# An opening rearranged: the first batch found by its least key, one-hot tables in pieces, later gathers, and scores tied to their own banks

## The chip, the cores and the metric

The kernel runs on one core of a Trainium2 chip. The metric is the device time of one execution in microseconds (us), the median of several runs. TensorE is called PE (PEld for its weight loads), VectorE DVE, ScalarE ACT, GpSimd POOL and SyncE SP.

## What is computed

Sixteen batches of 1024 tokens with 512 channels go through an attention with 8 heads of 64, in which query, key and value are the same projection, and a 0/1 mask per token decides which tokens take part. The result passes through a second projection and is added to the input.

```python
def _L0_cond_ref(x, mask, Wq, Wo):            # x: (16, 512, 1024), mask: (16, 1024)
    xt = jnp.transpose(x, (0, 2, 1))
    q = xt @ Wq.T
    qh = q.reshape(B, T, NH, dk).transpose(0, 2, 1, 3)
    scores = scale * jnp.einsum('bhqd,bhkd->bhqk', qh, qh)
    logits = (scores * cmask + (1.0 - cmask) * NEG) * rmask
    attn = jax.nn.softmax(logits, axis=-1)
    ctx = jnp.einsum('bhqk,bhkd->bhqd', attn, qh)
    out = ctx @ Wo.T
return x + jnp.transpose(out, (0, 2, 1))
```

About half of the tokens of a batch are masked in. A row whose token is masked out has equal logits, so its context is the mean over all tokens.

## The kernel before

**Only masked-in tokens are worked on.** For each batch the kernel computes a slot for every token, turns the slots into a list of row numbers, and gathers the masked-in rows by an indirect DMA. Some 512 tokens per batch (512 for the first and the last two batches, 544 or 528 between, with the rest as padding) then go through the projection, the scores, the exponentials and the value product. The mean row for the masked-out tokens comes from sums over the batch's natural layout.

**Batches are taken in another order than they come.** `order` (L202 to L210) counts each batch's tokens on PE, makes a key of the count times 32 plus the batch's number, and ranks the keys by comparing all 16 with all 16. The batch of rank 15 (the comparison counts larger keys, so the least key) is taken first. `permute` (L224, L227) picks a batch's mask out of all by comparing ranks with the place (`placed`, L215). `sources` (L234 to L237) does the same for the batch's number, from which come the row numbers' base and the address of the natural layout.

**From a mask to gathered rows.** `slots_of` (L295 to L316) forms prefix sums of the mask on PE (L300, L304) and turns them into slots on DVE, and the token table `oht`. `hot` (L360) makes the one-hot table `tmp` of 8 blocks of 128 in one DVE instruction. `index` multiplies the two on PE (L369), and DVE writes the row numbers `idx` (L372) and two padding masks (L384, L386). `gather` issues an indirect DMA of 128 rows on POOL (L458), 256 KB each. `xt` transposes the gathered rows on PE (L562), ACT and DVE split them into a high and a low half-precision part (L520, L521).

**From rows to scores.** `query` runs 12 products of 128 by 256 (L591) into one PSUM buffer of `pm`, of which there are two, and ACT copies the result (L595). `qsplit` splits it on DVE (L614 to L616) and SP spreads it over the partitions with four DMAs (`xx`, L625 to L628). `value` transposes it (L651). `scores(b, p, u)` works on batch b, head pair p and half u of the rows: 8 products (L823) fill four PSUM banks, then four exponentials on ACT read one bank each (L838). The first product of the next scores waits for all four of them (`self.left`):

```python
            if n == 0 and self.left:
                self.needs(m.ins, *self.left)
```

`attend` multiplies the probabilities with the values (L858, 32 products per head pair) into banks 4 and 5.

**The order.** In the opening (up to `self.begun.close()`) the calls stand in a list `first`, written by hand, and the tile framework places instructions by priority; `behind` and `needs` add dependences. PE is fed with idle products (`warm`, L408) while it waits for rows. From then on, PE's order is the one in which the calls stand in `plan`, by step of the batch. Where `self.paced` is set, gathers and scatters go into a queue, and each step issues one to two of them, held back to the last PE instruction so far (`self.beat`). Loads of weights and of the natural layout are issued by SP, whose instructions run in order, as do those of each engine.

In the opening before, batch 0 and batch 1 are both prepared first (`order`, `permute`, `sources(0, 2)`, `slots_of(0)`, `hot(0)`, `index(0)`, four gathers, then `permute(1, 2)`, `slots_of(1)`). Batch 1's index and its first four gathers stand in `first` between the first queries of batch 0.

Of the kernel before, what the change touches and what calls it, by code (L numbers as in the profile page):

```python
# [15 lines left out]
ALU = mybir.AluOpType  # L16
# [31 lines left out]
class Fast:  # L48
# [47 lines left out]
    def setup(self, mask_t):  # L96
# [44 lines left out]
        self.act16 = fixed("act16", [P, B, TB], F16)  # L141
        self.rank = fixed("rank", [P, B])
        self.base = fixed("base", [P, B])
        self.first_row = fixed("first_row", [1, B], I32)
# [53 lines left out]
    def order(self):  # L198

        nc, B = self.nc, self.B  # L200
        mh = self.given16
        nc.vector.tensor_scalar(mh, self.mt, 0.5, None, ALU.is_gt)  # L202
        pn = self.pm([P, B])
        for j in range(TB):
            nc.tensor.matmul(pn, lhsT=self.on16, rhs=mh[:, :, j], start=(j == 0), stop=(j == TB - 1))
        key = self.sb([P, B], F32, "sc", 3)
        nc.vector.scalar_tensor_tensor(key, pn, 32.0, self.number, ALU.mult, ALU.add)
        more = self.sb([P, B, B], F16, "c", 4)
        nc.vector.tensor_tensor(more, key.unsqueeze(1).broadcast_to([P, B, B]), key.unsqueeze(2).broadcast_to([P, B, B]), ALU.is_gt)
        nc.vector.tensor_reduce(self.rank, more, AX.X, ALU.add)  # L210
# [75 lines left out]
    def slots_of(self, b):  # L286


        nc = self.nc
        n = self.n[:, b:b + 1]  # L290
        mb = self.act16[:, b]
        whole, half = self.sb([P, 7, TB], F32, "c", 4), self.sb([P, TB, 2 * NB], F16, "c", 4)
        free, sign, put, base, slot, hi, far = (whole[:, k] for k in range(7))
# [12 lines left out]
        nc.vector.scalar_tensor_tensor(base, free, n, put, ALU.mult, ALU.add)  # L306
        nc.vector.tensor_tensor(slot, sign, pr, ALU.mult)
        nc.vector.tensor_tensor(slot, slot, base, ALU.add)
        nc.vector.tensor_tensor(ge, slot.unsqueeze(2).broadcast_to([P, TB, NB - 1]),
                                self.kk_kept.unsqueeze(1).broadcast_to([P, TB, NB - 1]), ALU.is_ge)  # L310
        nc.vector.scalar_tensor_tensor(far, ge[:, :, 4], float(5 * P - C), slot, ALU.mult, ALU.add)
        nc.vector.tensor_reduce(hi, ge, AX.X, ALU.add)
        nc.vector.scalar_tensor_tensor(self.lo[:, b], hi, -float(P), far, ALU.mult, ALU.add)
        nc.vector.tensor_tensor(oh, hi.unsqueeze(2).broadcast_to([P, TB, NB]),
                                self.ionb.unsqueeze(1).broadcast_to([P, TB, NB]), ALU.is_equal)
        nc.vector.tensor_tensor(self.oht[:, b], oh, self.tok.unsqueeze(2).broadcast_to([P, TB, NB]), ALU.mult)  # L316

# [470 lines left out]
    def scores(self, b, p, u):  # L788
# [26 lines left out]
        for j in range(max(map(len, lanes))):  # L815
            calls += [l[j] for l in lanes if j < len(l)]
        opening = b == 0 and p == 0 and u == 0
        if opening:
            calls.sort(key=lambda c: c[0] // (2 * A))
        banks = [c[0] // 512 for c in calls]  # L820
        for n, (c0, c1, w, x) in enumerate(calls):
            with self.behind(*last), self.tc.high_priority(offset=HPO if n else 0):
                m = nc.tensor.matmul(flat[:, c0:c1], lhsT=w, rhs=x, start=banks[n] not in banks[:n], stop=banks[n] not in banks[n + 1:])  # L823
            if out and banks[n] < 4:
                self.other_banks(m.ins, out)
            elif out and banks[n] not in banks[:n]:
                self.needs(m.ins, out)
            self.other_banks(m.ins, *self.spot_reads)
            if n == 0 and self.left:
                self.needs(m.ins, *self.left)  # L830
            last = [m.ins]
        self.beat = last[0]
        self.left, self.context_out = [], None
        ps = {}
        for j in (0, 1, 2, 3) if opening else (3, 0, 1, 2):
            k, i, at = places[j]
            t = self.sb([P, C], F32, "p", 12)[:, :A]
            e = nc.scalar.activation(t, flat[:, at:at + A], AF.Exp, bias=s["nm"][p // 2][:, p % 2 * 2 + k:p % 2 * 2 + k + 1],  # L838
                                     scale=SCALE, accum_out=s["z"][:, 2 * p + k, i:i + 1]).ins
            self.exp = [e]  # L840
            self.left.append(e)
            ps[k, i] = t
        s.setdefault("p", {}).setdefault(p, {}).update(ps)

    def attend(self, b, p, after=None):
# [7 lines left out]
        for g in (1, 0):  # L853
            cols = slice(g * CH, (g + 1) * CH)
            for i in range(3, -1, -1):
                for k in (1, 0):
                    with self.behind(*(first or ([after] if after else []))), self.tc.high_priority(offset=HPO):
                        mm = nc.tensor.matmul(pav[k * DK:(k + 1) * DK, g], lhsT=s["v"][p][:, i, k * DK:(k + 1) * DK],  # L858
                                              rhs=ps[k, i][:, cols], start=(i == 3), stop=(i == 0 and A == 512))
                    self.other_banks(mm.ins, *exps[1 - g:])  # L860
                    if g == 0 and i == 3:
                        self.needs(mm.ins, *exps[:1])
# [231 lines left out]
    def run(self, flag):  # L1094
# [128 lines left out]
        if True:  # L1223
            stack = ExitStack()
            for b in range(B + 1):
# [23 lines left out]
                if n < B:  # L1249
# [57 lines left out]
                for k, x in enumerate([x for x in (b + 2, self.extra.get(b + 2)) if x is not None and x < B]):  # L1307
# [186 lines left out]
```

## Time and profile before

| | us |
|---|---|
| three runs | 964.02, 964.62, 966.39 |
| median | 964.62 |
| the profiled execution | 965.21 |
| its span, first to last instruction | 963.5 |
| busy in the span: PE, DVE, ACT, POOL | 931.5, 721.1, 644.7, 305.1 |

A row of the timeline reads: start, duration, engine, line and operation, output and inputs with their shapes, count, and in brackets how long the engine was idle before it and what ended that. The waits list who waited for whom, with the total, the number of times and the longest. A row by stage gives the stage, its length, the busy time of each engine with the number of instructions, the clock granted to PE as a share, the DMA engines' share and the GB/s that they moved. An instruction's duration includes its latency: on DVE the next independent one starts some 0.1 us before the end that is shown.

### The profile page before, as it was taken

Reading aid. Unit: us, or ns where it says so; the run is one execution under the profiler, and the core shown is the slowest. Engines: PE = TensorE matmul, PEld = TensorE weight load, DVE = VectorE, ACT = ScalarE, POOL = GpSimd, SP = SyncE. Lnnn points to the kernel's source line nnn. Section 1 sums busy time; section 2 is a strip of 40 time slices with the busy share of each in tenths; the row PEclk is TensorE's granted clock in tenths of the full one; section 3 lists DMA queues with packets and bytes.
Section 4 is the critical chain, followed back from the end, with each engine's and each line's share of the span. In section 5 each row is a group of like instructions: output and inputs, shape, how many; then the busy total and the mean of one; then the engine's idle time right before and its main releaser. Section 6 shows DMA issues by size and latency. Waiting matters only on the chain.

```text
span 963.5 us, 22790 instructions
## 1 busy us (share of the span) xinstructions
PE 931.5 (97%) x8121; PEld 581.3 (60%) x8121; DVE 721.1 (75%) x2443; ACT 644.7 (67%) x1669; POOL 305.1 (32%) x311
## 2 busy tenths in 40 slices
PE   6799999999999999999999999999999999999997
PEld 4556656566666666666666566666666666565543
DVE  7779677776777767887678687877877788685563
ACT  4778766667677666776767678665767866665651
POOL 2102022142241513415144250522515135252452
PEclk9999999999999999999999999999999999999999
DMA  5756556556675666756656787654767757555552
GB/s 172 222 175 203 155 154 183 163 180 190 180 209 148 194 197 193 220 157 199 177 181 204 198 239 223 177 158 136 214 168 233 243 144 207 151 161 161 171 175 102
DMA packets 78568, 176.30 MB, mean 183 GB/s; under 512 B 14480, under 2 KB 22416, under 8 KB 78448
## 3 DMA queue, kind: packets, MB, share of 16 engines
q1 hardware_dynamic: 57392, 107.09, 39.8%
q0 software_dynamic: 21056, 67.68, 22.4%
q8 instruction: 66, 1.08, 0.5%
q14 instruction: 54, 0.44, 0.2%
HBM read 91.36 MB, written 33.91 MB: 130 GB/s over the span
## 4 chain that ended last, share of the span: by engine, by line
PE 81%; DVE 10%; ACT 4%; DMA 2%; issue 2%; SPq 1%; POOL 0%; POOLq 0%; DVEq 0%; ACTq 0%
PE pss L858 22%; PE pss L823 17%; PE pm L982 17%; PE pm L591 16%; ACT p L838 2%; PE pss L876 2%; PE pm L562 2%; DMA xx<-hl 1%; PE pss L766 1%; PE pm L654 1%; DVE xl L521 1%; PE pss L982 1%; DVE xa L988 1%; PE pm L912 1%; DVE p L777 1%
## 5 line engine op out<-in xcount | busy, mean ns | idle before, releaser
L838 ACT ACTIVATE p<-pss,nm 128x528 f32<-128x528 f32 (+2 forms) x512 | 353.9, 702 | 104.7 <-PE pss L823 101.5
L858 PE MATMUL pss<-p,v 128*64 128x264 f32 (+2 forms) x2048 | 242.4, 389 | 0.0
L823 PE MATMUL pss<-xx 128*128 128x118 f16 (+17 forms) x1856 | 213.6, 287 | 3.9 <-ACT p L838 2.8
L1051 POOL DMA_INDIRECT y_out<-xa,idx x68 | 82.0, 1206 | 405.2 <-DVE nq L732 85.1
L858 PEld LDWEIGHTS pss<-p,v 128*64 128x64 f32 x2048 | 141.4, 137 | 85.8 <-issue 4.9
L823 PEld LDWEIGHTS <-xx 128*128 128x128 f16 (+1 forms) x1856 | 103.2, 96 | 85.1 <-issue 34.3
L591 PE MATMUL pm<-xh,wqh 128*128 128x264 f16 (+5 forms) x512 | 141.8, 277 | 3.3 <-DVE xl L521 1.3
L591 PE MATMUL pm<-xh,wql 128*128 128x264 f16 (+5 forms) x512 | 141.1, 275 | 0.0
L591 PE MATMUL pm<-xl,wqh 128*128 128x264 f16 (+5 forms) x512 | 140.9, 275 | 0.0
L591 PEld LDWEIGHTS <-wqh 128*128 128x128 f16 x1024 | 96.4, 97 | 31.6 <-issue 12.6
L458 POOL DMA_INDIRECT xa<-x_in,idx x68 | 72.5, 1066 | 123.4 <-DMA y_out<-xa,idx 49.1
L838 ACT ACTIVATION_READ_ACCUMULATOR p<-pss,nm 128x1 f32 x512 | 105.2, 205 | 0.0
L982 PE MATMUL pm<-woh,ch 128*128 128x512 f16 x240 | 91.1, 380 | 0.0
L982 PE MATMUL pm<-woh,cl 128*128 128x512 f16 x240 | 90.9, 379 | 0.0
L982 PE MATMUL pm<-wol,ch 128*128 128x512 f16 x240 | 90.9, 379 | 0.0
L595 ACT ACTIVATE q<-pm 128x264 f32<-128x264 f32 (+5 forms) x128 | 50.8, 397 | 43.1 <-PE pm L591 42.7
L988 DVE SCALAR_TENSOR_TENSOR xa<-pm,xa 128x512 f32<-128x512 f32 x61 | 41.6, 681 | 46.0 <-PE pm L982 45.7
L1051 POOL DMA_INDIRECT y_out<-xi,idx x60 | 64.9, 1081 | 33.9 <-PE pss L766 13.4
L658 ACT COPY v<-pm 128x512 f32<-128x512 f32 x64 | 37.5, 586 | 56.0 <-PE pm L654 54.3
L982 PEld LDWEIGHTS <-ch 128*128 128x128 f16 x480 | 44.9, 98 | 47.5 <-issue 4.1
L458 POOL DMA_INDIRECT xi<-x_in,idx x60 | 59.4, 990 | 21.6 <-issue 15.8
L881 ACT COPY c<-pss 128x528 f32<-128x528 f32 (+2 forms) x64 | 38.3, 598 | 37.9 <-PE pss L876 26.8
(249 smaller groups left out, 1485.0 us busy)
## 6 DMA issues: line engine op xcount, KB each, us to landing
xm<-x_nat_in SPq DMA_DIRECT2D x60, 512.0 KB
xx<-hl SPq DMA_DIRECT2D x208, 136.0 KB
rb<-rd SPq DMA_DIRECT2D x72, 132.0 KB
xx<-hl SPq DMA_DIRECT2D x48, 128.0 KB
pt<-c SPq DMA_DIRECT2D x36, 132.0 KB
pt<-p SPq DMA_DIRECT2D x36, 132.0 KB
rb<-rd SPq DMA_DIRECT2D x32, 136.0 KB
ub<-ud SPq DMA_DIRECT2D x16, 256.0 KB
```

Source lines behind the costliest of these rows:

```text
L458: dma = self.nc.gpsimd.indirect_dma_start(out=tile[:n], out_offset=None, in_=self.x, in_offset=bass.IndirectOffsetOnAxis(ap=idx, axis=0))
L562: self.pe = nc.tensor.transpose(pt[:, c, :], x[:n, c * P:(c + 1) * P], self.ident[:n, :n]).ins
L591: self.beat = nc.tensor.matmul(pq, lhsT=w[:, c, e * P:(e + 1) * P], rhs=xx[:, c, cols], start=(k == 0), stop=(k == 3 * DC - 1)).ins
L595: nc.scalar.activation(s["q"][:, e, cols], pq, AF.Copy, scale=1.0 / (SX * SW))
L658: nc.scalar.copy(v, pv)
L823: m = nc.tensor.matmul(flat[:, c0:c1], lhsT=w, rhs=x, start=banks[n] not in banks[:n], stop=banks[n] not in banks[n + 1:])
L838: e = nc.scalar.activation(t, flat[:, at:at + A], AF.Exp, bias=s["nm"][p // 2][:, p % 2 * 2 + k:p % 2 * 2 + k + 1], scale=SCALE, accum_out ...
L858: mm = nc.tensor.matmul(pav[k * DK:(k + 1) * DK, g], lhsT=s["v"][p][:, i, k * DK:(k + 1) * DK], rhs=ps[k, i][:, cols], start=(i == 3), sto ...
L881: self.context_out = nc.scalar.copy(c[:, :A].rearrange("p (g c) -> p g c", g=2), pav).ins
L982: mm = nc.tensor.matmul(po[:cols.stop - cols.start], lhsT=a[:, e, cols], rhs=w[:, e, :], start=(e == 0 and k == 0), stop=(e == DC - 1 and ...
L988: return self.nc.vector.scalar_tensor_tensor(x, po, 1.0 / (SX * SW), x, ALU.mult, ALU.add).ins
L1051: dma = self.nc.gpsimd.indirect_dma_start(out=self.out, out_offset=bass.IndirectOffsetOnAxis(ap=idx, axis=0), in_=x, in_offset=None)
```

## The change

Four things are changed, all in the preparation and the work of batch 0 and in the preparation of batch 1.

1. `order` ends with the least of the 16 keys per partition; comparing the keys with it picks the first batch's mask directly. The comparison of all keys and the ranks (`ranks`) come later, and `sources` runs for batches 1 to 15 alone. The first batch's number is the least key minus 32 times its count, in `slots_of`.
2. `slots_of` now makes the one-hot table itself, with a DVE instruction for each block of 128, and forms the token table after the third. `hot` is no longer called for batches 0 and 1.
3. Batch 1's slots stand behind the second block of transposes, its index behind the first value block and the split of the first query, and all five of its gathers in the queue of the first step, behind the first scores. The weights of the second projection and the natural layout of later batches are held back to `self.beat` in place of the instruction `top` of batch 0's first shift. Four of batch 1's five blocks of transposes, in place of three, stand ahead of the first `attend`.
4. In batch 0, a score product waits for the exponential that reads its own bank, and an exponential for the products of its own bank; the exponentials are taken in the order in which the banks are complete. `attend` no longer waits for the bank-3 exponential where a row of scores has 512 columns.

The number of idle products on PE goes from 30 to 24.

```diff
     def order(self):
...
-        key = self.sb([P, B], F32, "sc", 3)
+        key = self.fixed("key", [P, B])
         nc.vector.scalar_tensor_tensor(key, pn, 32.0, self.number, ALU.mult, ALU.add)
+        self.key = key
+        nc.vector.tensor_reduce(self.least, key, AX.X, ALU.min)
+        each = self.sb([P, TB, B], F16, "hl", 2)
+        nc.vector.scalar_tensor_tensor(each, key.unsqueeze(1).broadcast_to([P, TB, B]), self.least,
+                                       mh.rearrange("p b j -> p j b"), ALU.is_equal, ALU.mult)
...
+            nc.vector.tensor_reduce(self.act16[:, 0], each, AX.X, ALU.add)
+
+    def ranks(self):
+        nc, B, key = self.nc, self.B, self.key
         more = self.sb([P, B, B], F16, "c", 4)
...
     def slots_of(self, b):
...
+        if b == 0:
+            who = self.base[:, 0:1]
+            nc.vector.scalar_tensor_tensor(who, n, -32.0, self.least, ALU.mult, ALU.add)
+            nc.vector.tensor_copy(self.first_row[:, 0:1], who[0:1, :])
+            nc.vector.tensor_scalar(who, who, float(T), None, ALU.mult)
...
-        nc.vector.tensor_tensor(self.oht[:, b], oh, self.tok.unsqueeze(2).broadcast_to([P, TB, NB]), ALU.mult)
+        for j in range(TB):
+            nc.vector.tensor_scalar(ol[:, j], self.io128, lo[:, j:j + 1], None, ALU.is_equal)
+            if j == 2:
+                nc.vector.tensor_tensor(self.oht[:, b], oh, self.tok.unsqueeze(2).broadcast_to([P, TB, NB]), ALU.mult)
...
     def scores(self, b, p, u):
...
-            if n == 0 and self.left:
+            if alone and self.left:
+                own = (1, 2, 3, 0)[banks[n]]
+                if banks[n] not in banks[:n]:
+                    self.needs(m.ins, self.left[own])
+                self.other_banks(m.ins, *(e for k, e in enumerate(self.left) if k != own))
+            elif n == 0 and self.left:
                 self.needs(m.ins, *self.left)
...
-        for j in (0, 1, 2, 3) if opening else (3, 0, 1, 2):
+        for j in done:
...
+            if alone:
+                self.other_banks(e, *(m for m, bank in zip(mms, banks) if bank != j))
...
     def attend(self, b, p, after=None):
...
-                    self.other_banks(mm.ins, *exps[1 - g:])
-                    if g == 0 and i == 3:
+                    self.other_banks(mm.ins, *exps[(1 - g) * (self.reach > 512):])
+                    if g == 0 and i == 3 and self.reach > 512:
                         self.needs(mm.ins, *exps[:1])
...
     def run(self, flag):
...
             self.order()
-            self.permute(0, 1)
-            self.active(0, 1)
-            self.sources(0, 2)
             self.slots_of(0)
-            self.hot(0)
-        self.warm(6)
+        self.warm(5)
         self.index(0)
         for j in range(4):
             self.gather(0, j)
-        self.warm(5)
+        self.warm(13)
         with self.behind(self.st[0]["at"], self.pe):
-            with self.tc.high_priority(offset=HPO):
-                self.permute(1, 2)
-                self.active(1, 2)
-                self.slots_of(1)
             for f in halves:
                 f()
-            with self.tc.high_priority(offset=HPO):
-                self.sources(2, B)
+            self.ranks()
+            self.permute(1, 2)
             self.setup2()
-        self.warm(13)
...
             self.warm(2)
+            if k == 1:
+                self.slots_of(1)
...
         def index1():
             with self.behind(self.last_xs):
-                self.hot(1)
+                self.sources(1, B)
                 self.index(1)
...
-        first = query(0, 0, 0) + xt(0)[3:] + [(0, L(self.facts, 0, 2))] + query(0, 1, 0) + query(0, 0, 1)
+        first = query(0, 0, 0) + xt(0)[3:] + query(0, 1, 0) + query(0, 0, 1)
...
-        first += [(0, index1)] + sums0[:4] + value(0, 0) + g1[:1] + query(0, 1, 1)[:1] + g1[1:2]
-        first += value(0, 1) + split1 + sums0[4:] + query(0, 2, 0) + g1[2:3] + query(0, 2, 1)[:1] + g1[3:4]
+        first += sums0[:4] + value(0, 0) + query(0, 1, 1)[:1] + [(0, index1), (0, L(self.facts, 0, 2))]
+        first += value(0, 1) + split1 + sums0[4:] + query(0, 2, 0) + query(0, 2, 1)[:1]
...
-                        plan = {(0, 0): g1[4:] + query(0, 3, 0) + value(0, 2) + rng0,
+                        plan = {(0, 0): g1 + query(0, 3, 0) + value(0, 2) + rng0,
                                 (3, 0): query(0, 3, 1) + x[:1] + value(0, 3) + pk(b, 1),
-                                (5, 0): x[1:3], (5, 1): x[3:],
+                                (5, 0): x[1:4], (5, 1): x[4:],
...
-                        free.setdefault(2, []).append(L(self.load, "o", c, None, first_top))
+                        free.setdefault(4, []).append(lambda c=c: self.load("o", c, None, self.beat))
...
-                        free.setdefault(at, []).append(L(self.load_all, x, c, None if b else first_top))
+                        free.setdefault(at, []).append(L(self.load_all, x, c) if b else lambda x=x, c=c: self.load_all(x, c, self.beat))
```

More of the change, by code (lines that the diff above doesn't have):

```diff
@@ L142, in setup @@
         self.rank = fixed("rank", [P, B])
+        self.least = fixed("least", [P, 1])
         self.base = fixed("base", [P, B])
@@ L205, in order @@
             nc.tensor.matmul(pn, lhsT=self.on16, rhs=mh[:, :, j], start=(j == 0), stop=(j == TB - 1))
-        key = self.sb([P, B], F32, "sc", 3)
+        key = self.fixed("key", [P, B])
         nc.vector.scalar_tensor_tensor(key, pn, 32.0, self.number, ALU.mult, ALU.add)
+        self.key = key
[3 more added lines that the diff above has]
+                                       mh.rearrange("p b j -> p j b"), ALU.is_equal, ALU.mult)
+        with nc.allow_low_precision(reason="one of the terms is 0 or 1, the others are 0"):
+            nc.vector.tensor_reduce(self.act16[:, 0], each, AX.X, ALU.add)
+    def ranks(self):
+        nc, B, key = self.nc, self.B, self.key
         more = self.sb([P, B, B], F16, "c", 4)
@@ L291, in slots_of @@
         mb = self.act16[:, b]
-        whole, half = self.sb([P, 7, TB], F32, "c", 4), self.sb([P, TB, 2 * NB], F16, "c", 4)
-        free, sign, put, base, slot, hi, far = (whole[:, k] for k in range(7))
+        whole, half = self.sb([P, 8, TB], F32, "c", 4), self.sb([P, TB, 2 * NB], F16, "c", 4)
+        free, sign, put, base, slot, hi, far, lo = (whole[:, k] for k in range(8))
         ge, oh = half[:, :, :NB - 1], half[:, :, NB:]
@@ L312, in slots_of @@
         nc.vector.tensor_reduce(hi, ge, AX.X, ALU.add)
-        nc.vector.scalar_tensor_tensor(self.lo[:, b], hi, -float(P), far, ALU.mult, ALU.add)
+        nc.vector.scalar_tensor_tensor(lo, hi, -float(P), far, ALU.mult, ALU.add)
+        ol = self.st[b]["ol"] = self.sb([P, TB, P], F16, "tmp", 2)
         nc.vector.tensor_tensor(oh, hi.unsqueeze(2).broadcast_to([P, TB, NB]),
                                 self.ionb.unsqueeze(1).broadcast_to([P, TB, NB]), ALU.is_equal)
-        nc.vector.tensor_tensor(self.oht[:, b], oh, self.tok.unsqueeze(2).broadcast_to([P, TB, NB]), ALU.mult)
+        for j in range(TB):
+            nc.vector.tensor_scalar(ol[:, j], self.io128, lo[:, j:j + 1], None, ALU.is_equal)
+            if j == 2:
+                nc.vector.tensor_tensor(self.oht[:, b], oh, self.tok.unsqueeze(2).broadcast_to([P, TB, NB]), ALU.mult)
     def facts(self, b0, b1):
@@ L816, in scores @@
             calls += [l[j] for l in lanes if j < len(l)]
-        opening = b == 0 and p == 0 and u == 0
-        if opening:
+        alone = b == 0
+        if alone and p == 0 and u == 0:
             calls.sort(key=lambda c: c[0] // (2 * A))
-        banks = [c[0] // 512 for c in calls]
+        banks, mms = [c[0] // 512 for c in calls], []
         for n, (c0, c1, w, x) in enumerate(calls):
@@ L828, in scores @@
             self.other_banks(m.ins, *self.spot_reads)
-            if n == 0 and self.left:
+            if alone and self.left:
[4 more added lines that the diff above has]
+            elif n == 0 and self.left:
                 self.needs(m.ins, *self.left)
             last = [m.ins]
+            mms.append(m.ins)
         self.beat = last[0]
-        self.left, self.context_out = [], None
+        self.left, self.context_out, self.reach = [], None, A
+        done = sorted(range(4), key=lambda j: len(banks) - banks[::-1].index(j)) if alone else (3, 0, 1, 2)
         ps = {}
-        for j in (0, 1, 2, 3) if opening else (3, 0, 1, 2):
+        for j in done:
             k, i, at = places[j]
@@ L841, in scores @@
             self.left.append(e)
+            if alone:
+                self.other_banks(e, *(m for m, bank in zip(mms, banks) if bank != j))
             ps[k, i] = t
+        if alone:
+            self.left = [self.left[done.index(j)] for j in (3, 0, 1, 2)]
         s.setdefault("p", {}).setdefault(p, {}).update(ps)
```

## The prediction

> **What bounds the kernel now.** I read the page's totals first, then busy time by stage, then who waits for whom, and last the timelines of the first 52 us, queue by queue. All times are us from the start of the span; a batch's score step is written (batch, head pair, half).
>
> ```profile
> span 963.5 us, 22790 instructions
> PE 931.5 (97%) x8121; PEld 581.3 (60%) x8121; DVE 721.1 (75%) x2443; ACT 644.7 (67%) x1669; POOL 305.1 (32%) x311
> 30.00:40.00 10.00, 6.84 (x44) 3.52 (x44) 6.94 (x25) 6.23 (x20) 2.59 (x3) 1.00 1.03 277
> 40.00:52.00 12.00, 9.81 (x77) 6.17 (x75) 7.78 (x19) 9.59 (x26) 0.00 (x0) 1.00 0.61 183
> 52.00:63.00 11.00, 11.00 (x98) 6.94 (x96) 7.83 (x30) 8.60 (x24) 0.00 (x0) 1.00 0.59 183
> 63.00:100.00 37.00, 35.09 (x335) 22.37 (x333) 35.96 (x129) 30.70 (x80) 5.01 (x5) 1.00 0.67 193
> 140.00:963.50 823.50, 808.09 (x7072) 503.64 (x7070) 611.34 (x2054) 549.19 (x1423) 282.06 (x261) 1.00 0.63 183
> ```
>
> A stage row gives its length, then busy time of PE, weight loads, DVE, ACT, POOL, then clock, DMA share and GB/s. After 140, PE is busy 98% of the time, so the change cannot speed anything there; it can only bring the start of that stretch forward. Between 30 and 52 PE is busy 16.65 of 22: 5.35 us of idle PE lie in the stage that the change edits. From 52 to 63 PE has no gap at all, and from 63 to 100 DVE is full. So the question is when PE reaches the point 51.63 (step (0,1,1)), and whether DVE lets that shift pass.
>
> ```profile
> PE pss L823 <- ACT p L838: 2.3, 2, 1.8
> PE pm L651 <- ACT q L595: 1.2, 3, 0.6
> PE pm L912 <- DVE xl L521: 1.1, 1, 1.1
> PE pss L823 <- DMA xx<-hl: 1.0, 1, 1.0
> DVE sc L262 <- PE pm L256: 1.5, 1, 1.5
> ```
>
> These are PE's largest waits from 14 to 52, and DVE's wait for the slot products of batches 2 and 3, at the edge of its full stretch. Scores wait for exponentials (2.3), for the spread of the query (1.0), for buffers. DVE itself waited 1.5 us for PE just before its full stretch, so that stretch starts when PE lets it: a shift of PE passes on whole.
>
> **The change, step by step: up to the first index.**
>
> ```profile
> 4.67 0.42 DVE L209 TENSOR_TENSOR c<-sc 128x256 f16<-128x256 f32 x1
> 6.29 0.29 DVE L227 TENSOR_REDUCE act<-hl 128x8 f16<-128x128 f16 x1
> 8.58 1.22 DVE L360 TENSOR_TENSOR tmp<-io,lo 128x1024 f16<-128x1024 f16 x1
> 10.39 0.23 DVE L372 TENSOR_SCALAR idx<-pm,base 128x9 int32<-128x9 f32 x1 [0.45 <-PE pm L369]
> 10.62 0.28 DVE L384 TENSOR_SCALAR hr<-row,n 128x128 f32<-128x128 f32 x1
> 10.81 0.38 DVE L224 TENSOR_TENSOR hl<-c,given 128x128 f16<-128x128 f16 x1
> 16.38 1.09 DVE L194 SCALAR_TENSOR_TENSOR wql<-xa,wqh 128x256 f16<-128x256 f32 x3
> 7.05 2.72 PE L408 MATMUL warm<-on 128*128 128x512 f16 x6
> 12.75 2.97 PE L408 MATMUL warm<-on 128*128 128x512 f16 x13
> 16.42 0.60 PE L562 MATMUL pss<-ident,xa 128*128 128x128 f32 x4
> 19.06 0.27 PE L591 MATMUL pm<-xl,wqh 128*128 128x256 f16 x1
> 17.06 0.60 ACT L520 ACTIVATE xh<-pss 128x512 f16<-128x512 f32 x1 [0.27 <-PE pss L562]
> L458 POOL DMA_INDIRECT xa<-x_in,idx x4: 942/988/1299, 10.9 to 15.1; - x4
> DMA to landing us min/median/max: 3.5/3.5/3.5
> L458 POOL DMA_INDIRECT xa<-x_in,idx x4: 942/957/979, 24.9 to 31.8; - x4
> DMA to landing us min/median/max: 5.1/5.1/5.1
> ```
>
> *Least key for the ranking.* From L209 to the last reduction L227 pass 6.29-4.67 = 1.62 us. In their place stand a reduction of 16 elements and a compare-and-multiply of 128. The second is like L384 or L224 (0.28 to 0.38), the first no longer than L227; together about 0.6. Gain 1.0. The three small instructions for the batch number fall into gaps between dependent instructions: 0 to 0.2 lost; I take 0.
>
> *One-hot in pieces.* L360 writes 1024 elements in 1.22. Eight pieces of 128 follow each other at 0.19 if each goes like L384 (10.62 to 10.81), 1.5 in all, so 0.3 is lost; if a piece costs half of that, 0.4 is won. PE may multiply while the later pieces come, which saves most of the 0.45 that DVE waited before L372. Between -0.6 and +0.3; I take -0.1, because L384 is the nearest row. The index is then ready at 9.3 instead of 10.39. [...]
>
> *Gathers and the transposes.* POOL starts four gathers 1.4 apart (10.9 to 15.1) and each lands 3.5 later. Moved by 1.1, the first lands at 13.3. It now overlaps the natural-layout loads: 0 to 0.5 lost. PE's 13 warm products start at 9.35; six of the first lot took 2.72 (0.45 each), the later thirteen 2.97 (0.23 each). If the fast rate comes at 12.75 as before, they end at 14.0. So the first transposes run at 14.0 instead of 15.55 and the second at 15.0 instead of 16.42.
>
> *Second batch's slots.* These now stand on PE between the second and third transposes, and wait for a mask that DVE gives only after its second low part. That comes at 15.0+0.64 (16.42 to 17.06 on ACT), +0.6 on ACT, +0.6 on DVE, +0.28 for L227 = 17.1. DVE is clear by then: eight weight splits of 0.34 (L194, three in 1.09) and the ranking end by 14. PE idles 1.2, so the first query half starts near 18.4 instead of 19.06: of 1.5 gained, 0.65 is left.
>
> **From the first query to step (0,1,1).**
>
> ```profile
> 22.71 0.27 PE L591 MATMUL pm<-xh,wqh 128*128 128x258 f16 x1
> 27.29 0.27 PE L591 MATMUL pm<-xh,wqh 128*128 128x256 f16 x1
> 25.89 0.69 DVE L615 TENSOR_TENSOR hl<-q,hl 128x512 f16<-128x512 f32 x1
> 28.73 0.60 SPq L628 DMA_DIRECT2D xx<-hl  x1
> 33.25 1.13 PE L823 MATMUL pss<-xx 128*128 128x512 f16 x4 [1.03 <-DMA xx<-hl]
> 34.42 0.69 ACT L838 ACTIVATE p<-pss,nm 128x512 f32<-128x512 f32 x1 [2.09 <-PE pss L823]
> 35.10 0.68 ACT L838 ACTIVATE p<-pss,nm 128x512 f32<-128x512 f32 x1
> 38.02 1.57 PE L823 MATMUL pss<-xx 128*128 128x512 f16 x8 [1.78 <-ACT p L838]
> 43.24 1.57 PE L823 MATMUL pss<-xx 128*128 128x512 f16 x8 [0.50 <-ACT p L838]
> 45.77 3.67 PE L858 MATMUL pss<-p,v 128*64 128x256 f32 x32
> 51.63 1.56 PE L823 MATMUL pss<-xx 128*128 128x512 f16 x8
> ```
>
> *Index of batch 1, later.* The second query half runs at 21.8 (was 22.71). DVE goes straight to the split of the query, since index, padding masks and tails no longer stand there: L615 at 24.5 instead of 25.89, and the last of its four spreads is issued at 27.3 instead of 28.73. That one landed at 33.25, 4.5 after issue, beside two gathers. Without them: 31.8 if nothing improves, about 30 if the load counted; I take 30.3. The price: PE now waits for the index work twice, and the third head pair's query starts at 27.45 instead of 27.29.
>
> *First scores.* They run without the 1.03 wait, from 30.45 to 32.0. The first exponential starts at 31.75 instead of 34.42, after ACT's sums over x: -2.7.
>
> *Bank ties dropped.* Before, step (0,0,1) waited for all four exponentials, the last of them behind two copies. Now four exponentials at 0.68 apart (34.42, 35.10) end at 34.5. PE has its other work (34.38 to 36.24 before, 1.86) done at 33.95 and follows them bank by bank: the scores end at 35.5 instead of 39.59, and ACT starts the next exponentials at 35.15 instead of the scores' end. These end at 37.85, the query copy and four transposes of the value follow, and (0,1,0) starts at 38.9 instead of 43.24: -4.3.
>
> *Batch 1's gathers, later.* They are tied to the end of the fourth query, 1.3 after the scores (the 1.86 less four transposes of 0.6), so at 33.3; they start 1.4 apart, and land 3.5 (alone) to 5.1 (beside other loads) after that: the fourth at 41.0 to 42.6 by rows, up to 43.5 if they also slow each other. Four of the five blocks of transposes, in place of three, now stand ahead of the first value product, so L858 waits for that landing: 42.8 to 44.0; I take 43.6, since weight loads run beside them. Before: 45.77, so -2.15.
>
> *Behind it.* From L858 to (0,1,1) took 5.86. One transpose of four moved ahead (0.6) and the 1.1 wait for DVE's low part goes, since that part is long done: 4.3. Step (0,1,1) starts at 47.9 instead of 51.63: **-3.7**. Other edits (attend's tie dropped in the last batches, fewer warm products) meet no wait: 0.
>
> The profiled execution took 965.21, span 963.5 and 1.71 around it; less 3.7 that is 961.5. The median of the three runs, 964.62, lies 0.6 below it, so I forecast 964.62-3.7 = 960.9.
>
> **Rivals.** 0.3% is 2.9 us, about what a measurement of this kernel can tell from no change.
>
> *Gathers late.* L858 waits for the fourth gather, and ahead of it no gather was waited for. In the 40 to 52 stage the engines moved 183 GB/s; with half of it for the gathers, 256 KB takes 2.9 us, so with the first at 38.5 the fourth lands at 47.1 and L858 starts near 47.2: (0,1,1) at 51.5, a gain of 0.1 or, at the 277 GB/s of 30 to 40 (1.9 each, 44.2), of 3.0. Middle: 963.1. For it: the 5.1 row, and weights, spreads and gathers now leave together; against: before, the spreads had that load and cost only 1.0. [...]
>
> *Nothing arrives.* The full DVE stretch from 63 takes the shift back, if its inputs are DMA loads and not PE. Against it stands the 1.5 us that it waited for PE. 964.6.
>
> *Slower.* A sum over batch 1's natural-layout load stands on ACT ahead of the exponentials of (0,1,1), and SP issues that load now behind the weights and the fourth spread. Those exponentials started at 51.63+1.56 = 53.2; the sum takes about 1.2 (L360's size on another engine, an estimate), so it decides from a landing at 52.0. By rows it lands near 48. If queues behind the weights add 7 us, it lands at 55, and the time is 967.6.
>
> **Chances and range.** Forecast 0.6 (959.4 to 961.7: gathers alone and cheap pieces give -5.2, late ones -2.9), gathers late 0.22, nothing arrives 0.08, slower 0.1. The range 959.4 to 964.1 takes in the forecast and most of the second case. Faster by over 0.3% is the forecast with the edge of the second: 0.62; within: 0.29; slower: 0.09.
>
> **What would show it.** Right: index by 9.5; no wait for the spread at the first scores; (0,0,1) starting before the fourth exponential ends; L858 at 42.8 to 44; (0,1,1) at 47 to 48.7; the same distance from there to the end. Wrong: the first value product or ACT ahead of (0,1,1) waiting for a DMA past 46 or 49, or DVE idle between 63 and 100 where it was full.

## The result, and the profile after

The changed kernel took 969.34 us (median of 8 runs, 966.27 to 972.99) beside 964.31 us of the kernel before (8 runs, 962.56 to 966.39): ratio 1.0053, 95% interval 1.0035 to 1.0071. In a second comparison (e8 below) it was 968.82 beside 964.11, 1.0040 [1.0025, 1.0056]. The forecast of 960.9 was wrong in sign.

The page's totals and busy time by stage of the changed kernel, columns as in the prediction (stage, length, PE, weight loads, DVE, ACT, POOL, clock, DMA share, GB/s):

```profile
span 967.2 us, 22795 instructions
PE 935.7 (97%) x8115; PEld 582.7 (60%) x8115; DVE 719.8 (74%) x2455; ACT 645.8 (67%) x1669; POOL 305.1 (32%) x311
30.00:40.00 10.00, 8.05 (x56) 4.47 (x55) 7.67 (x29) 8.09 (x25) 4.14 (x4) 1.00 0.59 132
40.00:52.00 12.00, 9.31 (x49) 5.17 (x49) 5.07 (x11) 5.58 (x13) 0.89 (x1) 0.72 0.92 284
63.00:100.00 37.00, 33.46 (x314) 21.45 (x311) 32.85 (x118) 28.39 (x76) 4.81 (x5) 1.00 0.71 202
```

From 30 to 40 PE is busy 8.05 instead of 6.84: the gain is there. From 40 to 52 it is busy 9.31, but with 49 products where 77 ran before, and the clock is 0.72 instead of 1.00. From 63 to 100 another 1.6 us of PE are lost (35.09 before), and DVE is no longer full. The waits of PE from 14 to 140, and of DVE and ACT from 52 to 140 (total, times, longest; `xm` is a piece of the natural layout, whose loads are called x loads below):

```profile
PE pm L582 <- DMA xa<-x_in,idx: 4.6, 2, 2.7
DVE ms L522 <- DMA xm<-x_nat_in: 3.6, 2, 2.3
ACT xm L515 <- DMA xm<-x_nat_in: 2.7, 2, 2.4
```

Before, PE never waited for a gather here. The timelines of POOL, SP and PE show how it comes about (start, length; in brackets the idle time before it and what ended it):

```profile
34.69 0.95 POOL L478 DMA_INDIRECT xa<-x_in,idx  x1 [20.52 <-DVE hl L636]
38.80 0.94 POOL L478 DMA_INDIRECT xa<-x_in,idx  x1 [0.30 <-issue]
37.71 2.25 SPq L185 DMA_DIRECT2D xi<-wo_in  x4
30.80 2.20 PE L843 MATMUL pss<-xx 128*128 128x512 f16 x8
34.69 1.56 PE L843 MATMUL pss<-xx 128*128 128x512 f16 x8
39.63 0.63 PE L582 MATMUL pm<-ident,xa 128*128 128x128 f32 x4 [1.95 <-DMA xa<-x_in,idx]
40.53 2.57 PE L843 MATMUL pss<-xx 128*128 128x512 f16 x8
47.39 0.84 PE L582 MATMUL pm<-ident,xa 128*128 128x128 f32 x4 [2.69 <-DMA xa<-x_in,idx]
48.15 5.10 PE L889 MATMUL pss<-p,v 128*64 128x256 f32 x32
53.71 1.56 PE L843 MATMUL pss<-xx 128*128 128x512 f16 x8
```

Step (0,0,1) starts at 34.69 (38.02 before), without a wait. Then PE waits for the first and for the fourth gather of batch 1. The fourth is started at 38.80, in the midst of four loads of the output weights that SP issues from 37.71 to 39.96, and PE can use it only at 47.39. The scores of (0,1,0) take 2.57 instead of 1.57 and the first value product 5.10 instead of 3.67. Step (0,1,1) starts at 53.71, 2.08 later than before. The clock column, us by us, says why those products are long:

```profile
40.00:41.00 1.00, 1.00 (x9) 0.72 (x8) 0.08 (x1) 0.71 (x2) 0.89 (x1) 0.92 1.05 306
41.00:42.00 1.00, 1.00 (x3) 0.15 (x1) 1.00 (x2) 0.37 (x1) 0.00 (x0) 0.50 1.07 356
42.00:43.00 1.00, 1.00 (x5) 0.13 (x4) 1.00 (x4) 0.24 (x1) 0.00 (x0) 0.50 1.00 383
43.00:44.00 1.00, 1.00 (x7) 0.97 (x6) 0.90 (x4) 1.00 (x3) 0.00 (x0) 0.50 1.12 418
44.00:45.00 1.00, 0.69 (x5) 0.46 (x3) 0.20 (x2) 1.00 (x4) 0.00 (x0) 0.87 0.99 341
```

What is missing from 1.00 in these five rows is 0.08+3 x 0.50+0.13 = 1.71, so the half clock lasted 3.42 us. A second such stretch lies between 47 and 52 (0.83, three times 0.50 and 0.96).

As a mark behind all this I take the last tail scores of batch 0, on PE, of the kernel before and of the changed one:

```profile
89.00 0.65 PE L766 MATMUL pss<-xx 128*32 128x272 f16 x16
92.86 0.65 PE L786 MATMUL pss<-xx 128*32 128x272 f16 x16
```

The mark is 3.86 late and the span 3.7 longer, so nothing is gained or lost behind it. From (0,1,1) to the mark passed 37.37 before and 39.15 now: that is where the waits for xm lie.

### The profile page after: what moved, and what is told of

The parts are those of the page before. It is cut to its first block, busy times and chain, and to the rows that moved or that the text cites. A ratio compares the mean times of both kernels' runs of the same rounds, so it can differ in the third digit from the quotient of the medians.

```text
span 967.2 us, 22795 instructions
## 1 busy us (share of the span) xinstructions
PE 935.7 (97%) x8115; PEld 582.7 (60%) x8115; DVE 719.8 (74%) x2455; ACT 645.8 (67%) x1669; POOL 305.1 (32%) x311
## 4 chain that ended last, share of the span: by engine, by line
PE 79%; DVE 7%; ACT 4%; DMA 4%; issue 1%; SPq 1%; POOL 0%; POOLq 0%; DVEq 0%; ACTq 0%
PE pss L889 22%; PE pm L1013 16%; PE pss L843 16%; PE pm L611 15%; PE pss L907 2%; ACT p L865 2%; PE pm L582 2%; DMA xm<-x_nat_in 2%; PE pss L786 1%; PE pm L674 1%; DVE xl L541 1%; DMA xa<-x_in,idx 1%; DMA xx<-hl 1%; PE pss L1013 1%; ACT xm L515 1%
## 5 line engine op out<-in xcount | busy, mean ns | idle before, releaser
L615 ACT ACTIVATE q<-pm 128x264 f32<-128x264 f32 (+5 forms) x128 | 50.9, 398 | 43.6 <-PE pm L611 43.4
```

Source lines behind the costliest of these rows:

```text
L615: nc.scalar.activation(s["q"][:, e, cols], pq, AF.Copy, scale=1.0 / (SX * SW))
```

## The experiments

**First comparison.** e1 to e4 ran on a chip on which the kernel before took 981.72 us (median of 35 runs), so only ratios and places in the traces count.

e1: batch 1's gathers back among the queries.

```
+ first += g1[:2] + value(0, 1) + ... + query(0, 2, 0) + g1[2:3] + query(0, 2, 1)[:1] + g1[3:4]
- plan = {(0, 0): g1 + query(0, 3, 0) ...
+ plan = {(0, 0): g1[4:] + query(0, 3, 0) ...
```

> The changed kernel with one part undone: batch 1's gathers are again issued among the queries behind its index (two behind it, one behind query(0,2,0), one more, the tail's at the first step of the plan). Late-gathers theory: POOL starts them at 27 to 31 instead of 34.69 to 40.05, the fourth lands by about 40, both PE waits for them (1.95 and 2.69 us) go and with them the stretches of half clock (about 3.3 us in the scores, the transposes and the first attend), so (0,1,1) starts at 46 to 48 instead of 53.71 and the time is 961 to 964. Contention theory (the gathers were worth moving because they slow the first spreads): the first scores' second half and the first exps come 1 to 3 us later, (0,0,1) starts at 36 to 38, and the time stays at 966 to 970.

Ratio 0.9985 [0.9955, 1.0015]. Both waits for a gather are gone, the value product starts at 45.16 and takes 3.67:

```profile
26.64 0.98 POOL L478 DMA_INDIRECT xa<-x_in,idx  x1 [12.44 <-DVE idx L392]
44.57 0.66 PE L582 MATMUL pm<-ident,xa 128*128 128x128 f32 x4 [1.57 <-DVE xl L541]
49.29 1.56 PE L843 MATMUL pss<-xx 128*128 128x512 f16 x8
```

(0,1,1) is 4.4 earlier than in the changed kernel. (0,0,1) stands at 35.42, 0.7 later than there; that is not harm from the gathers beside the spreads, since e6 below, with the same gathers, has it at 34.59. Of the time itself the interval says little. A wait of 1.57 for DVE's low part has taken the gathers' place.

e2: weights and x loads at their places of before.

```
- free.setdefault(4, []).append(lambda c=c: self.load("o", c, None, self.beat))
+ free.setdefault(2, []).append(L(self.load, "o", c, None, first_top))
- ... L(self.load_all, x, c) if b else lambda x=x, c=c: self.load_all(x, c, self.beat)
+ ... L(self.load_all, x, c, None if b else first_top)
```

> The changed kernel with one part undone: the output weights are loaded from step 2 and the x loads of batch 0's steps are released by the first shift again, not by the product at hand. Queue theory: the waits of VectorE and ScalarE for xm in 52 to 100 us fall from 3.6 and 2.7 to about 1 and PE wins back the 1.6 us it lost between 63 and 100: time 967 to 968. Contention theory: the weights go out beside the gathers, the fourth gather lands later than 47.3, (0,1,1) comes at 55 or later and the time is 970 to 973. If the loads' place doesn't matter: 969.3.

Ratio 1.0028 [0.9995, 1.0062]. (0,1,1) at 53.89, the mark at 91.33, 37.44 behind it: so from (0,1,1) to the mark it is as before, and the queue theory holds by these places; the interval of the ratio says little. The value product took even longer, 6.15, most of it at half clock (0.73 from 40 to 52).

```profile
46.27 1.09 PE L582 MATMUL pm<-ident,xa 128*128 128x128 f32 x4 [2.34 <-DMA xa<-x_in,idx]
```

Three of the four weight loads went out at 30.95 here, long before the gathers, but two x loads followed the fourth gather (38.51) at 38.81, and PE got it only 1.1 earlier than in the changed kernel. So it is not the weights alone that hold it up.

e3: ties back.

```
- alone = b == 0
+ alone = False
```

> The changed kernel with one part undone: the first product of a block of scores waits for all exps of the block before again, and an exp for the whole block. Late-gathers theory: (0,0,1) starts 3 us later, at about 38, but the gathers start at the same time and the fourth lands at about 47, so PE's waits for the gathers shrink by what the wait at 38 takes; (0,1,1) at 53 to 54 and the time within 1.5 us of 969.3. If the dropped ties still pay in full at the end: 972 to 973.

Ratio 1.0013 [0.9983, 1.0043]. (0,0,1) starts at 37.54, yet (0,1,1) at 51.45, 2.3 earlier than in the changed kernel and 1.5 earlier than expected, and the mark at 93.70, behind a stretch of half clock from 86 to 89 (0.95 over 63 to 100; 16 score products from 85.87 on take 3.02, their like in e12 1.71 to 1.78). With late gathers the dropped ties are worth nothing: what PE gains, it waits. Here its waits are of other kinds, and the clock stays at 1.00 to 52.

```profile
46.73 0.66 PE L582 MATMUL pm<-ident,xa 128*128 128x128 f32 x4 [1.12 <-DVE xl L541]
```

The fourth gather starts at 39.35, and the weights, released by the product at hand, leave only at 41.41: with the weights behind the gather, PE waits for no gather.

e4: products that nobody reads, in the two waits.

```
+ for _ in range({0: 9, 3: 12}.get(k, 0) if b == 1 else 0):
+     nc.tensor.matmul(pt, lhsT=self.on16, rhs=..., start=True, stop=True)
```

> The changed kernel with 9 products that nobody reads ahead of the transposes of batch 1's first block and 12 ahead of those of its fourth, into the tile that the transposes then overwrite; they fill the waits of 1.95 and 2.69 us. Idle-clock theory: the granted clock stays near 1 from 40 to 52 us, scores(0,1,0) take 1.6 instead of 2.57 us and the first attend 3.7 instead of 5.10, (0,1,1) starts at 50 to 51 instead of 53.71 and the time is 966 to 967. If the half clock comes from something else than the waits: the rows stay at 2.57 and 5.10 and the time is 969 to 970.

Ratio 1.0067 [1.0037, 1.0096]. The clock is 1.00 and the value product 3.67, as the idle-clock theory has it, but the time is not: the order on ACT and DVE came out another way, and the sum of xm stands ahead of the fourth block's split.

```profile
52.20 1.06 ACT L515 ACTIVATE xm<-xm 128x1024 f32<-128x1024 f32 x1 [5.33 <-DMA xm<-x_nat_in]
55.23 0.33 PE L946 MATMUL pm<-ident,rcol 128*128 128x128 f32 x1 [2.26 <-DVE xl L541]
```

That is the mechanism of the rival "Slower", a sum on ACT that waits for a late x load. In the changed kernel itself that first sum runs at 53.95 without waiting for its load, so the rival's price was not paid there; ACT's waits for xm come later (0.30 until 59.33, 2.40 until 67.89).

**Second comparison** (the kernel before: 964.11, 31 runs).

e5: e4's products and e2's loads together.

> e4's products and e2's loads together: the waits for the gathers are filled and the x loads go out early. In e4 the clock stayed at 1.00 and the first attend took 3.67 us, but the sums of xm stood ahead of the fourth block's split on ScalarE and VectorE and waited for a load that landed at 52.2. With the loads early that wait is gone. Clock theory: (0,1,1) starts 2 to 3 us before e2's 53.89, at 51 to 52, and the last tail scores of batch 0 start 37.4 us later, at 88.5 to 89.5 (e2 91.33). If the half clock only filled a wait that is there anyway: (0,1,1) at 53.5 to 54 again.

964.96 us, ratio 1.0004 [0.9995, 1.0014].

```profile
40.00:52.00 12.00, 10.62 (x76) 6.04 (x75) 6.11 (x12) 7.23 (x17) 0.62 (x1) 1.00 0.98 284
51.76 1.56 PE L846 MATMUL pss<-xx 128*128 128x512 f16 x8
```

(0,1,1) at 51.76 instead of e2's 53.89: with the loads early, the half clock costs 2.1 us, by one trace of each on two chips. It is a cost of the waits, and comes on top of them.

e6: e1's gathers and e2's loads together.

> The changed kernel with two parts undone: e1's gathers among the queries and e2's loads at their places of before; the opening and the dropped ties stay. If gathers and loads are the whole loss: (0,1,1) at 48 to 49.5, the last tail scores of batch 0 37.4 later, at 85.5 to 87 (before 89.00, changed 92.86), and the time 2 to 4 us under the kernel before, ratio 0.996 to 0.998. Contention theory (gathers, spreads and weights together slow the first batch): (0,1,1) at 51 or later and no gain on before.

962.57 us, ratio 0.9984 [0.9973, 0.9995]; (0,1,1) at 49.60, the mark at 87.04. The loss was gathers and loads, and turns into a gain, of 1.5 us where 2 to 4 were expected.

e7: e6 with ties and the fourth block's place of before, so the opening alone.

```
- (5, 0): x[1:4], (5, 1): x[4:],
+ (5, 0): x[1:3], (5, 1): x[3:],
```

> e6 with the ties to all exps back and the fourth block of batch 1 behind the attend again: only the opening (least key, ranks later, table in pieces) is left of the change. If the dropped ties pay: (0,0,1) starts at 37.5 to 38, (0,1,1) 2 to 3 us later than e6, and the last tail scores at 88 to 89.5. If the waits on ScalarE's q and VectorE's xl (1.07 and 1.57 us in e1) take the ties' place: (0,1,1) within 1 us of e6 and the last tail scores with it.

963.29 us, ratio 0.9991 [0.9980, 1.0001]; (0,1,1) at 50.20, the mark at 87.41, only 0.4 behind e6. The value product starts at the same 44.33 in both, first e6 with its wait, then e7:

```profile
43.74 0.66 PE L582 MATMUL pm<-ident,xa 128*128 128x128 f32 x4 [1.57 <-DVE xl L541]
44.33 3.67 PE L889 MATMUL pss<-p,v 128*64 128x256 f32 x32
36.58 1.57 PE L843 MATMUL pss<-xx 128*128 128x512 f16 x8 [1.79 <-ACT p L865]
44.33 3.67 PE L889 MATMUL pss<-p,v 128*64 128x256 f32 x32
```

e6 has (0,0,1) 2.0 earlier and loses it again with the fourth block ahead of the value product.

e8: the changed kernel again.

> The changed kernel itself, beside the three others on one chip. If the profile of it is typical: half clock again between 40 and 52 us, (0,1,1) at 53 to 55, the last tail scores of batch 0 at 92 to 94, ratio to the kernel before 1.003 to 1.007. If the waits for the gathers were an accident of one execution: (0,1,1) at 51 to 52 and a ratio of 1.000 to 1.002.

968.82 us, ratio 1.0040 [1.0025, 1.0056]. The profile, which is of the longest run (972.27), shows the same picture, worse: three waits of 7.2 in all, the fourth block at 49.08, clock 0.69 between 40 and 52.

```profile
49.08 1.09 PE L582 MATMUL pm<-ident,xa 128*128 128x128 f32 x4 [3.75 <-DMA xa<-x_in,idx]
```

It is not an accident of one execution. Over all their runs the mean granted clock of the changed kernel was 0.9954 (0.9961 when it was first measured), that of the kernel before 0.9987: 0.0033 of 965 us is 3.2 us of clock.

**Third comparison** (the kernel before: 964.44, 31 runs).

e9: e6 with the fourth block behind the value product again (e7's second edit alone).

> e6 with the fourth block of batch 1 back behind the first attend, as in the kernel before; opening and dropped ties stay. In e6 the fourth block's transposes wait 1.57 us for the xl of an earlier block, and the attend starts at 44.33, as late as in e7 without the dropped ties. If that place eats the ties' gain: the attend starts at 42 to 42.8, (0,1,1) at 48 to 48.8 (e6 49.60, before 51.63), the last tail scores at 85.4 to 86.2, and the time 2.5 to 3.5 us under before. If the wait is for the split whatever stands there: (0,1,1) within 0.5 us of e6.

962.53 us, ratio 0.9981 [0.9970, 0.9991]. The value product starts at 42.06 and (0,1,1) at 48.38, as expected, but the mark only at 87.40 (85.4 to 86.2 was expected), and the time is 1.9 under before instead of 2.5 to 3.5: behind a wait of 1.53 the clock halved again.

```profile
48.21 0.33 PE L943 MATMUL pm<-ident,rcol 128*128 128x128 f32 x1 [1.53 <-DVE xl L541]
50.00:51.00 1.00, 1.00 (x6) 0.36 (x3) 0.43 (x1) 0.75 (x3) 0.00 (x0) 0.50 0.77 284
```

e10: the kernel before with the dropped ties alone.

> The kernel before with only the scores and the attend of the changed one (ties to exps of other banks dropped). If the ties pay by themselves when the fourth block stands behind the attend: (0,0,1) starts at 36 to 36.5 instead of 38.02, (0,1,1) 1.3 to 2.2 us earlier than 51.63 and the time 1 to 2 us under before. If they only move the wait to ScalarE's q or the split: (0,1,1) within 0.5 us of 51.63 and the ratio within 0.001 of 1.

962.45 us, ratio 0.9983 [0.9968, 0.9997], (0,1,1) at 48.61. The profile caught its longest run (967.68), so its mark says nothing. It shows something else: the first product of the program starts when DVE has made `given` from the mask, in this trace (second row) a microsecond earlier than in that of the kernel before (first row).

```profile
3.94 0.41 PE L205 MATMUL pm<-given,on 128*128 128x16 f16 x8 [3.94 <-DVE given L202]
2.99 0.41 PE L205 MATMUL pm<-given,on 128*128 128x16 f16 x8 [2.99 <-DVE given L202]
32.21 1.13 PE L823 MATMUL pss<-xx 128*128 128x512 f16 x4 [0.95 <-DMA xx<-hl]
```

In all profiles but e3's and that of the kernel before it starts at 2.90 to 3.01; in those two DVE took 1.15 and 1.06 for the mask, in the changed kernel 0.23. The execution of before that was profiled took 965.21, above every median of that kernel but that of e1 to e4 (the others: 963.17 to 964.62). On an equal footing its marks are 0.95 earlier: (0,1,1) at 50.7, the tail scores at 88.05.

e11: the changed kernel with the gathers released by the first scores.

```
- plan = {(0, 0): g1 + query(0, 3, 0) ...
+ plan = {(0, 0): g1 + [(0, self.issue)] * 5 + query(0, 3, 0) ...
```

> The changed kernel with batch 1's gathers released by the last product of the first scores, as the prediction had taken it (first at 33.3), and not by the last product of query(0,3,0) (34.69). If the start is the mis-sized term: each gather lands 1.4 us earlier, PE's waits for them fall from 4.6 by 1.4 to 2.8 us, and the time is 966 to 967.5. If the landings are set by what else moves (spreads, weights, x loads) and not by the start: the fourth still lands at 46.5 to 48.5, and the time is within 1 us of the changed kernel's.

964.08 us, ratio 1.0000 [0.9991, 1.0008]. (The prediction had the fourth query's end as release, and put it at 33.3.)

```profile
37.29 0.95 POOL L478 DMA_INDIRECT xa<-x_in,idx  x1 [0.30 <-issue]
37.53 1.95 SPq L185 DMA_DIRECT2D xi<-wo_in  x4
43.76 0.63 PE L582 MATMUL pm<-ident,xa 128*128 128x128 f32 x4 [1.67 <-DMA xa<-x_in,idx]
48.45 1.57 PE L843 MATMUL pss<-xx 128*128 128x512 f16 x8
```

The fourth gather starts 1.5 earlier, now just ahead of the weights, and PE has it 3.6 earlier, more than either theory allowed; the clock stays at 1.00 to 52. By the ratios this one release is worth 4 to 5 us.

e12: e9 with the weights late again.

> e9 with the output weights alone at step 4 and released by the product at hand, as in the changed kernel; the x loads stay early. If the late x loads alone cost the time between 63 and 100: as e9, within 0.5 us. If the weights in their new place push the x loads behind them in SP's queue: the sums wait for xm again, the last tail scores come 1 us or more after e9's.

961.73 us, ratio 0.9971 [0.9961, 0.9982], the best of all.

```profile
42.01 3.67 PE L889 MATMUL pss<-p,v 128*64 128x256 f32 x32
47.85 1.57 PE L843 MATMUL pss<-xx 128*128 128x512 f16 x8
85.28 0.65 PE L786 MATMUL pss<-xx 128*32 128x272 f16 x16
```

The mark is 2.1 ahead of e9's, whose stretch of half clock is missing here. The weights' new place costs nothing when the gathers are early; of the two loads that e2 moved back, the x loads were the ones that cost time behind 63.

**Alone, with the kernel before at 963.17 (9 runs).** e13: the weights wait for the fourth gather.

```
+ if (b, j) == (1, 3): self.fourth = self.pool[0]
- self.load("o", c, None, self.beat)
+ self.load("o", c, None, self.fourth)
```

> The changed kernel with one release changed: the output weights' loads wait until the fourth gather of batch 1 has landed, and not only for the product at hand; the gathers start at the same time as in the changed kernel (34.7 to 40.1). Collision theory (the four weight transfers, issued at 37.71 ahead of the fourth gather at 38.80, hold that gather back): the fourth block's transposes start at 43.5 to 45 instead of 47.39, PE's waits for the gathers fall from 4.6 to 2 to 3 us in all, and the time is 965 to 967. Start theory (the gathers land some 8.5 us behind their start whatever is beside them, so e11 won by its earlier start alone): the transposes stay at 46.5 to 48, and since the weights and x loads come later the time is 969 or more.

966.84 us, ratio 1.0038 [1.0025, 1.0052].

```profile
45.48 0.63 PE L584 MATMUL pm<-ident,xa 128*128 128x128 f32 x4 [1.27 <-DMA xa<-x_in,idx]
37.52 0.34 SPq L532 DMA_DIRECT2D xm<-x_nat_in  x1
43.00:44.00 1.00, 0.78 (x8) 0.54 (x6) 0.71 (x2) 0.83 (x3) 0.00 (x0) 1.00 0.18 58
44.00:45.00 1.00, 0.21 (x2) 0.00 (x0) 0.82 (x2) 0.76 (x2) 0.00 (x0) 1.00 0.10 41
```

From nearly the same start (38.60) the fourth block comes at 45.48, between the two theories; the waits fall only to 4.1. The collision is real (1.9 us earlier than in the changed kernel, 3.6 than in e8), but one x load of 512 KB slipped into the weights' place, so its whole size stays open. Nor is traffic all of it: from 43 to 45 the DMA engines are busy for 0.18 and 0.10 of the time, and PE still waits for the last of the gather until 45.48. The time is lost behind: x loads come later still, and from (0,1,1) at 50.17 to the mark pass 40.85.

## Why the prediction was wrong

**What the parts are worth, on an equal footing** (mark against 88.05; time against the kernel before of the same comparison): opening alone (e7) -0.6, time -0.8; ties alone (e10) (0,1,1) -2.1, time -2.0; both, with gathers and x loads early (e12) -2.8, time -2.7; the changed kernel +4.8, time +5.0. So what the change could bring is 2.7, and the changed kernel lies 7.7 behind that. The moved gathers and loads are some 6.5 of it: e6, which has them early but keeps the fourth block ahead of the value product, is 1.5 under before. By the mark the gathers alone give back 5.3 (e1), the loads alone 1.5 (e2), both together 5.8 (e6).

**Up to the first index: right.** Predicted 10.39 to 9.3; measured 8.45 with the mask ready 1.0 early, so 9.4 to 9.5. The one-hot pieces overlap PE's products as assumed; five take 0.90, so they follow each other at some 0.17, near the 0.19 of L384. The -5.2 at the low end of the range counted on pieces at half of 0.19, which no run shows.

**First transposes: too large.** Predicted 1.55 earlier; 14.60 in e10 against 13.65 here is 0.95. The 13 warm products took 5.55, 0.43 each: the fast rate that the sum set in at 12.75 did not come, though the clock column reads 1.00 there.

**Index of batch 1, later: the cost was mis-sized.** By the second query half 0.65 of the opening's gain is left (21.11; before, on an equal footing, 21.76), where 0.9 was predicted. The third head pair's query starts at 27.26, which looks like the predicted 27.45; on an equal footing before had it at 26.33, so it is 0.93 late and not 0.16. The eight products of the first scores then take 2.20 at one stretch, where 1.55 was taken, the time of later scores; before, the same eight took 0.38, 0.91 and 1.13 in three pieces. They end at 33.00 (predicted 32.0), while e10, with the opening of before, ends them at 32.21+1.13 = 33.34. That no spread is waited for was right, but it brought 0.34 instead of 2.4, because PE itself came to the scores late.

**Bank ties: right in the mechanism.** (0,0,1) starts without waiting for exps, and in e10 the dropped ties alone bring 2.0 there (35.03; before, on an equal footing, 37.07). In e12 (0,1,1) stands at 47.85 (predicted 47.9), with the gathers out of the way and the fourth block behind the value product, but that agreement is luck: 47.9 was reckoned from the trace with the late mask, and on an equal footing e12 gains 2.8 and not 3.7.

**The fourth block ahead of the value product: no price was set.** The prediction moved its 0.6 and let the wait of 1.1 behind the value product go. In e6 the value product comes 2.3 later than in e9 (44.33 and 42.06), since the block's transposes wait for DVE's low part (1.57).

**Batch 1's gathers: the step that failed.** Start 34.69 instead of 33.3, as the scores end 1.0 later and the release took 0.4 more. Landing was put at 41.0 to 43.5 by rows of gathers that had been issued well ahead of the weights (the 5.1 is that of a gather at 29.82, with two weight loads at 32.25); here the fourth started among them and was used at 47.39, 8.6 after its start. The value product then started at 48.15 and not at 43.6: that is 4.6 of the 5.8 by which (0,1,1) came later than predicted (53.71 and 47.9). The rival "Gathers late" had this landing (47.1) to 0.3, at 0.22, but in part by luck: it took half of 183 GB/s, while the engines moved 284 between 40 and 52, and for nearly that rate (277) it gave 44.2. No run shows that the gathers get half of what is moved; from start to use the fourth took 8.6 here and 6.9 in e13 (38.60 to 45.48), where one x load stood in the weights' place. And the rival put (0,1,1) at 51.5, without what the waits do to the clock.

**Half clock: not in the sum.** The attend took 5.10 and the scores of (0,1,0) 2.57; e5 against e2 prices it at 2.1. The stretch from the value product to (0,1,1), 5.56, less 1.43 for the clock, is 4.1 where 4.3 was predicted, so the clock accounts for the 1.3 that remain of the 5.8.

**"The same distance from there to the end": wrong by 1.8.** The sum followed the x loads only up to ACT's first sum. Their release by the product at hand put all of batch 0's loads later (39.15 against 37.37; 37.43 in e12).

## What to carry to other kernels

The fourth gather, moved behind a compute step, left among four loads that SP issued from 37.71 to 39.96, and was used 8.6 us after its start, where the sum had 3.5 to 5.1 from other stretches: look up what SP sends in that window before taking a landing time from another stretch. Where PE's work is short of its data, reckon with the clock as well: in the changed kernel a stretch of half clock took 1.7 us of PE's time on top of the wait, and it came behind a wait of 1.53 us (e9) and not behind one of 1.95 (e13). And before a sum of differences is made against one profiled execution, see when its first product started: here 0.95 us of the apparent distance lay ahead of it, where DVE took 1.06 for the mask instead of 0.23.

## What was not expected of the hardware

The granted clock halved behind waits of PE of 1.53 us (e9), of 1.95 and 2.69 (changed kernel), and of 0.62 and 1.01 with 0.33 of work between them (e3), and stayed at 1.00 behind others as long: 1.57 (e6), 1.78 (the kernel before), 1.95 (e13). The half clock lasted 3.42 us in the rows shown, and as long in the second stretch of the changed kernel, which begins 6.8 behind the start of the first (47.66 and 40.84), twice that length. Reckoned in the same way from the clock by stage, and so to a few tenths, it lasted 3.3 in e9 (0.88 from 40 to 52, 0.98 from 52 to 63), 3.7 in e3 (0.95 from 63 to 100), 6.9 in e2 (0.73 from 40 to 52, 0.98 from 52 to 63) and 10.3 in e8 (0.69 and 0.87 there): near one, two and three times one length. No run shows what sets this length, and which waits halve the clock was not settled.
